# A diagonal LSTM and a quantum convolution on one core: preparation rounds and a part of the first statistics put on ScalarE, aggregation on Pool, and a pause in the circuit's preparation

## The chip, the cores and the metric

The kernel runs on one core of a Trainium2 chip. The metric is the device time of one execution in microseconds (us). Three runs of the kernel before gave 1410.7, 1411.99 and 1412.01 us; their median is 1411.99 us.

## What is computed

The input `x` has 16 images of 128 channels and 64 x 64 pixels, in float32 (33.5 MB). Two layers follow each other, and each adds its result to its input:

```python
x = x + _L0_conv_ref(_gn(x), w_is, b_is, w_ss, b_ss)
x = x + _L1_conv_ref(_gn(x), pre_w, pre_b, q_weights, post_w, post_b)
```

`_gn` is a group norm with 32 groups of 4 channels: mean and variance over 4 channels and all pixels of an image. The first layer is a diagonal LSTM. The rows are skewed (row i shifted right by i), and a scan runs over the 127 diagonals; at each, all rows take one LSTM step in which a row's gates depend on its own state and on that of the row above:

```python
s_s = einsum(w_ss[:, :, 0], h_shift) + einsum(w_ss[:, :, 1], h) + b_ss
o, f, ig = split(sigmoid(gates[:, :3 * C])); g = tanh(gates[:, 3 * C:])
c_new = f * c + ig * g
h_new = o * tanh(c_new)
```

A skewed row is zero where it has no pixel. The second layer projects each pixel's channels to 4 angles, simulates a circuit of 4 qubits with fixed weights, and projects its 4 expectations to 128 channels.

## The kernel before, in words

Channels lie on the partitions. The kernel has three stages, and each engine works through its instructions in the order in which the program issues them, because all three are written under a manual schedule.

**Preparation.** `rows(b)` and `behind(b)` (L247 to L264) issue on SP's queue the loads of image b: 40 rows go into the buffer `ring`, 24 more in three chunks of 512 elements into `rest` or `spare` buffers. `statistics(b, k)` (L285) takes the sums of one chunk of 512 elements on VectorE (`bn_stats`), eight chunks for each image, and `aggregated(b)` (L289) joins the eight into the image's mean and variance per channel (`mv1`, `bn_aggr`). Beside this, 33 rounds of `inv_step` (L190) work out the LSTM states of a row in the steps ahead of its first pixel, where the input is zero and all images and positions have the same state. A round is one chain: 4 matmuls of the state column `hinv[:, j]` with the summed weights `wsT`, 4 gate activations on ScalarE (L202, in the order f, i, g, o), three tiny operations on Pool (L205 `f*c`, L206 `i*g`, L207 their sum, the new cell state in `cinv`), then a tanh (L209) and the product with o (L210) on ScalarE, which gives the next column of `hinv`. After each round two extra matmuls `keep` (L179) run on TensorE with results that nobody reads; the first reads a piece of image b in `ring`. The loop over b (from L375) issues 2 or 3 rounds ahead of the statistics of each image; `between` puts two small weight preparations after the sixth and seventh round.

The end of the preparation, in TensorE's order: Pool copies columns of `hinv` into the first state (L402, L403), 8 matmuls start the gates of step 0 (L408), three `keep` matmuls follow, then the matmul of `group_mean` (L147) with `mv1` of all images, the variance's matmul (L426), and, when VectorE and ScalarE have made `mean1` and `rstd1`, the input matmuls of step 0 (L597).

**The scan.** `step(t)` runs 160 times; rows are handled in two bands of 32, so that a slot that ends a row of the first goes on with a row of the second. A step is three weight products for each of four gates (L783), the sum of two halves (`add`, L798), activations (L802), the cell update (L850 to L861), tanh (L862) and the new state (L868). The input product of a later step (`gate_ps`, L597) stands behind it on TensorE. Pool normalises the input (L576 to L588) and adds the result to `ring` (L641). Beside this VectorE does two side jobs. One is `statistics(us, now)` (L716), which takes from the list `waiting` as many `bn_stats` (L732) of finished rows as fit a budget, for the second norm; `pieces(g)` says at which column a block of four rows comes onto the list: at column 64 for the first eight blocks, in two halves for those of the second band. The other is the circuit's preparation, `steps = circuit(cur)`: 120 small operations (L441, L452, L466, L483) that fill `w_amp`; each step t above 32 draws three of them (`next(steps, None)`, L814 to L816).

**The second layer** runs over the images (L1011 to L1062) and stores the output.

Of the kernel before, what the change touches and what calls it, by code (L numbers as in the profile page):

```python
# [11 lines left out]
F32 = mybir.dt.float32  # L12
AF = mybir.ActivationFunctionType
# [3 lines left out]
P = 128  # L17
NB = 16
NH = 64
NW = 64  # L20
SLOTS = 32
PAIRS = SLOTS // 2
NC = PAIRS * NB
RING = 40
ROWS = 4
BLOCK = ROWS * NW
CHUNK = 2 * BLOCK
EARLY = 33
FIRST = 8
STRIP = 4  # L30
FEW = 96
# [3 lines left out]
BAND = NW + 1  # L35
# [6 lines left out]
GO, GF, GI, GG = 0, 1, 2, 3  # L42
FUNC = {GO: AF.Sigmoid, GF: AF.Sigmoid, GI: AF.Sigmoid, GG: AF.Tanh}
# [38 lines left out]
def kernel(  # L82
# [16 lines left out]
    nc = tc.nc  # L99
# [10 lines left out]
    ring = const.tile([P, NB, RING * NW], F32, name="ring")  # L110
# [21 lines left out]
    w_amp = const.tile([P, 2, 128], F32, name="w_amp")  # L132
# [3 lines left out]
    def place(r):  # L136

        return (r + AHEAD if r < SLOTS else r - SLOTS) * NW
# [21 lines left out]
    small = ctx.enter_context(tc.tile_pool(name="small", bufs=2))  # L160
    with ExitStack() as scan:
# [29 lines left out]
        def inv_step(j, pool):  # L191


            ps = {}
            rhs = hinv[:, j : j + 1].to_broadcast([P, P])
            for g in ORDER:
                ps[g] = pool.tile([P, P], F32, name=f"inv_ps{j}_{g}", tag=f"inv{g}")
                w = wsT[:, g * 128 : (g + 1) * 128]
                nc.tensor.matmul(ps[g], lhsT=w, rhs=rhs, start=True, stop=True)
            ac = small.tile([P, 4], F32, name=f"inv_a{j}", tag="inv_a")  # L200
            for g in ORDER:
                nc.scalar.activation(ac[:, g : g + 1], ps[g][:, 0:1], FUNC[g], bias=bias[:, g : g + 1])  # L202
            ig = small.tile([P, 2], F32, name=f"inv_i{j}", tag="inv_i")
            c = cinv[:, j + 1 : j + 2]
            nc.gpsimd.tensor_mul(ig[:, 0:1], ac[:, GF : GF + 1], cinv[:, j : j + 1])  # L205
            nc.gpsimd.tensor_mul(ig[:, 1:2], ac[:, GI : GI + 1], ac[:, GG : GG + 1])  # L206
            nc.gpsimd.tensor_add(c, ig[:, 0:1], ig[:, 1:2])  # L207
            th = small.tile([P, 1], F32, name=f"inv_t{j}", tag="inv_t")
            nc.scalar.activation(th, c, AF.Tanh)  # L209
            nc.scalar.activation(  # L210
                hinv[:, j + 1 : j + 2], th, AF.Identity, scale=ac[:, GO : GO + 1]
            )

        def above(v, a, b):

# [4 lines left out]
        with ExitStack() as prep:  # L220
# [5 lines left out]
            ps_keep = prep_ps.enter_context(tc.tile_pool(name="ps_keep", bufs=1, space=PSUM))  # L226
# [11 lines left out]
            mv1 = pp.tile([P, NB, 2], F32, name="mv1")  # L238
# [46 lines left out]
            def statistics(b, k):  # L285
                v = ring[:, b, k * CHUNK : (k + 1) * CHUNK] if k < 5 else rests[b][k - 5]
                nc.vector.bn_stats(stats[:, b, k, :], v)

            def aggregated(b):  # L289
                nc.vector.bn_aggr(  # L290
                    mv1[:, b, :], stats[:, b, 0:8].rearrange("p g s -> p (g s)")
                )


            q3 = qw.rearrange("p (n a) -> p a n", a=3)
            ang = pp.tile([P, 2, 3, 8], F32, name="ang")
            rnd = pp.tile([P, 2, 3, 8], F32, name="rnd")
# [73 lines left out]


            between = [angle_weights, output_weights]
            done = 0
            for b in range(NB):  # L375
                while b < NB - 1 and done * (NB - 1) < EARLY * (b + 1):
                    inv_step(done, ps_inv)
                    keep(ps_keep, "keep", ring[:, b, CHUNK : CHUNK + P])
                    keep(ps_keep, "keep", wsT[:, 0:P])
                    if done == 0:  # L380

                        transposed("wxT", wxT, lambda g: wx_n[:, g, :])
                        transposed("w0T", w0T, lambda g: ws_n[g // 2][:, g % 2, 0::2])
                        transposed("w1T", w1T, lambda g: ws_n[g // 2][:, g % 2, 1::2])
                    elif done > 4 and between:
                        between.pop(0)()
                    done += 1
                if b + 2 < NB:
                    rows(b + 2)
                if b + 1 < NB:  # L390
                    behind(b + 1)
                    for k in ORDERED:
                        statistics(b + 1, k)
                for k in (5, 6, 7):
                    statistics(b, k)
                aggregated(b)
            prep_ps.close()


# [20 lines left out]
            var = pp.tile([P, NB], F32, name="var1")  # L420
# [4 lines left out]
            ps = ps_small.tile([P, NB], F32, name="gv1", tag="small")  # L425
# [347 lines left out]
        def step(t, ps):  # L773

            a, b = columns(t)
            few = plain(t)
            a0, b0 = wide(t, LEAST // 2 if few else LEAST)
# [71 lines left out]
            c = cst[:, :, a:w]  # L849
# [21 lines left out]
            s = t + 1  # L871
# [220 lines left out]
    with tc.manual_schedule():  # L1092
# [8 lines left out]
        th = bank(ps_t, "theta1")  # L1101
# [78 lines left out]
```

## Time and profile before

| | us |
|---|---|
| median of three runs | 1411.99 |
| the profiled execution, its own time | 1411.93 |
| its span on the core | 1409.8 |
| preparation, to the first input product of step 0 (L597) | 104.0 |
| start of the first state product (L783) | 106.8 |
| TensorE busy, of the span | 1355.0 (96%) |
| VectorE busy | 975.5 (69%) |
| ScalarE busy | 776.0 (55%) |
| Pool busy | 887.6 (63%) |

The profiled execution's own time is 2.1 us above its span. In what follows a "timeline" is the list of instructions in order of time; its columns are the start in us, the duration in us, the engine, the line, the operation, the tile that is written and those that are read, the shape, the number of merged instructions and, in brackets, the idle time of the engine ahead of it with what ended that. PE is TensorE, DVE VectorE, ACT ScalarE, POOL GpSimd; PEld is TensorE's load of weights. The "chain of waits" goes back from the last instruction, at each step to what released it. A float32 matmul shows as two records.

### The profile page before, as it was taken

What the parts mean: (1) busy time and instruction counts of PE and PEld (TensorE: products, weight loads), DVE (VectorE), ACT (ScalarE), POOL (GpSimd) and SP (SyncE); (2) the same over time, 40 slices, a digit from 0 to 9 for tenths busy, and PEclk for the clock granted to TensorE, in tenths of its full rate; (3) what the DMA queues carried; (4) which work ended last, traced back from release to release, by engine and by line L of the source; (5) the groups of instructions that cost most, each with busy time, mean ns of one, the idle gap of its engine ahead of it and who ended that gap; (6) DMA issues with size and microseconds to landing.
All of it is one profiled execution on the core that took longest, in us unless ns stands there. A gap on an engine that the chain in (4) does not pass through costs nothing.

```text
span 1409.8 us, 20064 instructions
## 1 busy us (share of the span) xinstructions
PE 1355.0 (96%) x6046; PEld 967.6 (69%) x6046; DVE 975.5 (69%) x2541; ACT 776.0 (55%) x1852; POOL 887.6 (63%) x1599
## 2 busy tenths in 40 slices
PE   6778999999999999999999999999999999999995
PEld 5658977777777766666677767777776787886332
DVE  7973565566665666887777776666665567876996
ACT  4655666555555555555555555555555566654331
POOL 4225777777777766777777776777777677763300
PEclk9999999999999999999999999999999999999998
DMA  9960000000000000133333100000000000014999
GB/s 339 407 234 2 1 1 1 1 0 1 0 1 1 1 1 1 60 120 120 120 120 120 60 1 1 1 1 0 1 1 0 1 0 1 1 31 143 383 400 358
DMA packets 64075, 107.04 MB, mean 76 GB/s; under 512 B 5040, under 2 KB 32720, under 8 KB 63968
## 3 DMA queue, kind: packets, MB, share of 16 engines
q1 hardware_dynamic: 59328, 94.39, 18.5%
q0 software_dynamic: 3408, 10.58, 2.0%
q8 instruction: 48, 0.79, 0.2%
q10 hardware_dynamic: 1232, 0.80, 0.2%
q14 instruction: 59, 0.48, 0.1%
HBM read 59.61 MB, written 46.14 MB: 75 GB/s over the span
## 4 chain that ended last, share of the span: by engine, by line
PE 82%; DVE 4%; ACT 1%; issue 1%; POOL 1%; DVEq 0%; ACTq 0%; POOLq 0%
PE ps L783 46%; PE ps L597 28%; PE po_None L1062 3%; PE theta_None L1011 2%; PE am_None L1040 1%; DVE spare L868 1%; DVE ps L858 1%; DVE ps L798 0%; DVE cst L861 0%; DVE stats L732 0%; ACT g L862 0%; ACT g L802 0%; PE po L1062 0%; DVE cst L850 0%; DVE ring L1080 0%
## 5 line engine op out<-in xcount | busy, mean ns | idle before, releaser
L597 PE MATMUL ps<-spare,wxT 128*128 128x512 f32 (+18 forms) x1280 | 479.7, 518 | 0.6 <-POOL spare L588 0.6
L798 DVE TENSOR_TENSOR ps<-ps,both 128x256 f32<-128x256 f32 (+9 forms) x536 | 219.1, 410 | 301.1 <-PE ps L783 299.5
L802 ACT ACTIVATE ps<-ps,bias 128x512 f32<-128x512 f32 (+23 forms) x480 | 279.1, 583 | 221.1 <-DVE ps L798 184.8
L783 PE MATMUL ps<-spare,w1T 128*128 128x256 f32 (+16 forms) x1272 | 346.8, 354 | 9.6 <-DVE spare L759 5.0
L597 PEld LDWEIGHTS ps<-spare,wxT 128*128 128x128 f32 x1280 | 231.1, 190 | 173.0 <-issue 155.4
L783 PE MATMUL ps<-spare,w0T 128*128 128x256 f32 (+16 forms) x1272 | 344.0, 352 | 0.0
L833 ACT COPY both<-ps 128x256 f32<-128x256 f32 (+9 forms) x536 | 189.6, 356 | 181.3 <-PE ps L783 161.7
L783 PEld LDWEIGHTS ps<-spare,w1T 128*128 128x128 f32 x1272 | 230.6, 190 | 36.5 <-DVE spare L868 7.2
L783 PEld LDWEIGHTS ps<-spare,wsT 128*128 128x128 f32 x1088 | 196.1, 190 | 80.4 <-DVE spare L868 30.1
L783 PE MATMUL ps<-spare,wsT 128*128 128x256 f32 (+14 forms) x1088 | 243.9, 366 | 2.6 <-DVE spare L868 1.2
L783 PEld LDWEIGHTS ps<-spare,w0T 128*128 128x128 f32 x1272 | 230.5, 190 | 21.0
L641 POOL TENSOR_TENSOR ring<-ring,spare 128x256 f32<-128x256 f32 (+15 forms) x375 | 231.5, 644 | 17.9 <-DVE spare L868 17.9
L588 POOL TENSOR_TENSOR spare<-spare,rstd 128x512 f32<-128x512 f32 (+10 forms) x160 | 170.9, 1068 | 14.8 <-DVE rstd L158 2.3
L582 POOL TENSOR_TENSOR spare<-ring 128x256 f32<-128x256 f32 (+13 forms) x165 | 139.8, 847 | 0.0
L862 ACT ACTIVATE g<-cst 128x256 f32<-128x256 f32 (+20 forms) x320 | 102.9, 368 | 65.5 <-DVE cst L861 65.1
L868 DVE TENSOR_TENSOR spare<-g,ps 128x256 f32<-128x256 f32 (+17 forms) x319 | 105.3, 368 | 44.8 <-ACT g L862 40.2
L576 POOL TENSOR_TENSOR spare<-ring,mean 128x256 f32<-128x256 f32 (+15 forms) x191 | 122.9, 644 | 5.6 <-DVE mean L148 5.4
L631 POOL TENSOR_TENSOR spare<-spare 128x240 f32<-128x240 f32 (+9 forms) x136 | 102.7, 755 | 36.4 <-DVE spare L868 32.8
L888 POOL COPY spare<-spare 128x16 f32<-128x16 f32 x64 | 21.0, 329 | 150.9 <-DVE spare L868 150.9
L802 ACT ACTIVATE g<-ps,bias 128x512 f32<-128x512 f32 (+20 forms) x160 | 97.3, 608 | 26.6 <-DVE ps L798 20.5
L861 DVE TENSOR_TENSOR cst<-cst,ps 128x256 f32<-128x256 f32 (+20 forms) x320 | 104.6, 368 | 5.5
L858 DVE TENSOR_TENSOR ps<-ps,g 128x512 f32<-128x512 f32 (+20 forms) x160 | 95.0, 594 | 18.8 <-ACT g L802 18.2
(370 smaller groups left out, 1096.4 us busy)
## 6 DMA issues: line engine op xcount, KB each, us to landing
out_dram<-ring SPq DMA_DIRECT2D x93, 256.0 KB, 4.8
ring<-in_x_dram SPq DMA_DIRECT2D x32, 512.0 KB, 7.6
low<-ring SPq DMA_DIRECT2D x6, 2048.0 KB, 7.5
ring<-in_x_dram SPq DMA_DIRECT2D x6, 2048.0 KB, 8.1
spare<-in_x_dram SPq DMA_DIRECT2D x27, 256.0 KB, 6.3
rest<-in_x_dram SPq DMA_DIRECT2D x21, 256.0 KB, 6.4
ring<-low POOLq DMA_DIRECT2D x18, 256.0 KB, 6.7
ring<-in_x_dram SPq DMA_DIRECT2D x16, 256.0 KB, 7.1
```

What stands on the lines that cost most here:

```text
L576: op = nc.gpsimd.tensor_sub(by_pairs(xn, 0, j0, j1), x0, over(mean1, j1 - j0))
L582: op = nc.gpsimd.tensor_sub(by_pairs(xn, 1, j0, j1), lower, of)
L588: nc.gpsimd.tensor_mul(v, v, r)
L597: nc.tensor.matmul(ps[g][:, :, a:b], lhsT=wxT[:, g * 128 : (g + 1) * 128], rhs=xns[t % 2][:, :, a:b], start=t > 0, stop=True, skip_group_c ...
L641: op = engine.tensor_add(x1, x1, by_pairs(new, q, j0, j1))
L783: nc.tensor.matmul(out, lhsT=w[:, g * 128 : (g + 1) * 128], rhs=rhs, start=False, stop=True, skip_group_check=True,)
L798: nc.vector.tensor_add(v, v, both[g][:, a:b])
L802: nc.scalar.activation(to[:, :, a:w], ps[g][:, :, a:w], FUNC[g], bias=bias[:, g : g + 1])
L833: nc.scalar.copy(both[g][:, a:b], ps[g][:, 0, a:b])
L858: nc.vector.tensor_mul(ig, ig, act[GG][:, :, a:w])
L861: nc.vector.tensor_add(c[:, q], c[:, q], ig[:, q])
L868: nc.vector.tensor_mul(new[:, q, a:v], th[:, q, a:v], act[GO][:, q, a:v])
```

## The change

Four things are changed. In `inv_step` the products `i*g` and the sum move from Pool to one ScalarE activation (scale i, bias `f*c`); Pool keeps `f*c`, now issued right after the gate f. For images 1 to 4 (`aside`) the chunk k = 0 is no longer taken by `bn_stats` but by two ScalarE activations with accumulated sums (`moments_of`), issued after the rounds of that image, and a third that writes the mean. For images 1 to 12 `bn_aggr` is left out, and Pool joins the eight entries of four images at a time (`gathering`), in pieces of which one is issued after each round (`some`); what is left when the rounds are over is issued after the loop over the images. And the circuit draws its three operations at the steps 33 to 62 and from 106 on, instead of from 33 on without a pause. Two smaller edits go with it: `coefficients()` is issued later on Pool, and the first `keep` after a round reads `wsT` instead of `ring`.

```diff
+GATHER = 4
@@ inv_step
+            kept = small.tile([P, 1], F32, name=f"inv_k{j}", tag="inv_k")
+            c = cinv[:, j + 1 : j + 2]
...
             for g in ORDER:
-                nc.scalar.activation(ac[:, g : g + 1], ps[g][:, 0:1], FUNC[g], bias=bias[:, g : g + 1])
-            ig = small.tile([P, 2], F32, name=f"inv_i{j}", tag="inv_i")
-            c = cinv[:, j + 1 : j + 2]
-            nc.gpsimd.tensor_mul(ig[:, 0:1], ac[:, GF : GF + 1], cinv[:, j : j + 1])
-            nc.gpsimd.tensor_mul(ig[:, 1:2], ac[:, GI : GI + 1], ac[:, GG : GG + 1])
-            nc.gpsimd.tensor_add(c, ig[:, 0:1], ig[:, 1:2])
...
+                activate(ac[:, g : g + 1], ps[g][:, 0:1], FUNC[g], bias=bias[:, g : g + 1])
+                if g == GF:
+                    nc.gpsimd.tensor_mul(kept, ac[:, GF : GF + 1], cinv[:, j : j + 1])
+            activate(c, ac[:, GG : GG + 1], AF.Identity, scale=ac[:, GI : GI + 1], bias=kept)
+            activate(th, c, AF.Tanh)
+            activate(hinv[:, j + 1 : j + 2], th, AF.Identity, scale=ac[:, GO : GO + 1])
@@ preparation
+            aside = range(1, 1 + GATHER)
...
+            def moments_of(b):
+                at = place(SLOTS)
+                v, x0 = ring[:, b, at : at + CHUNK], ring[:, b, at : at + 1]
+                junk = ps_small.tile([P, CHUNK], F32, name=f"junk{b}", tag="small")
+                for k, func in enumerate((AF.Identity, AF.Square)):
+                    nc.scalar.activation(
+                        junk, v, func, bias=x0, scale=-1.0, accum_out=sums1[:, k, b : b + 1]
+                    )
+                nc.scalar.activation(
+                    entries[:, b, 0:2, 1],
+                    sums1[:, 0, b : b + 1].to_broadcast([P, 2]),
+                    AF.Identity,
+                    bias=x0,
+                    scale=-1.0 / CHUNK,
+                )
+
+            def gathering(b0):
...
+                if b0 in aside:
+                    nc.gpsimd.tensor_mul(s1, s1, s1)
+                    nc.gpsimd.tensor_scalar_mul(s1, s1, -0.5 / CHUNK)
+                    yield
+                    nc.gpsimd.tensor_scalar_mul(s2, s2, 0.5)
+                    nc.gpsimd.tensor_add(
+                        inners[:, :, 0:2], *(v.unsqueeze(2).to_broadcast(pair) for v in (s1, s2))
+                    )
+                    yield
...
+                def total(to, v):
+                    n = 8
+                    while n > 1:
+                        nc.gpsimd.tensor_add(gathered[:, :, 0:n], v[:, :, 0:n], v[:, :, n : 2 * n])
+                        v, n = gathered, n // 2
+                        yield
+                    nc.gpsimd.tensor_add(to.unsqueeze(2), v[:, :, 0:1], v[:, :, 1:2])
+                    nc.gpsimd.tensor_scalar_mul(to, to, 1.0 / 16)
+                    yield
+
+                yield from total(m, means)
+                nc.gpsimd.tensor_sub(gathered, means, m.unsqueeze(2).to_broadcast([P, GATHER, 16]))
+                nc.gpsimd.tensor_mul(gathered, gathered, gathered)
+                yield
+                nc.gpsimd.tensor_scalar_mul(within, inners, 1.0 / BLOCK)
+                nc.gpsimd.tensor_add(gathered, gathered, within)
+                yield
+                yield from total(var, gathered)
...
-            coefficients()
             for v in (*hst, *xns, none):
                 nc.gpsimd.memset(v, 0.0)
             nc.gpsimd.memset(w_image, 0.0)
 
             for k in (3, 4, 0):
                 statistics(0, k)
+            coefficients()
...
+            behind_pool = []
+
+            def some():
+                for later in behind_pool[:1]:
+                    if next(later, True) is not None:
+                        behind_pool.pop(0)
+
             for b in range(NB):
                 while b < NB - 1 and done * (NB - 1) < EARLY * (b + 1):
                     inv_step(done, ps_inv)
-                    keep(ps_keep, "keep", ring[:, b, CHUNK : CHUNK + P])
+                    some()
+                    keep(ps_keep, "keep", wsT[:, 0:P])
                     keep(ps_keep, "keep", wsT[:, 0:P])
...
+                if b in aside:
+                    moments_of(b)
...
                     for k in ORDERED:
-                        statistics(b + 1, k)
+                        if k or b + 1 not in aside:
+                            statistics(b + 1, k)
                 for k in (5, 6, 7):
                     statistics(b, k)
-                aggregated(b)
+                if b in (0, *range(13, NB)):
+                    aggregated(b)
+                if b in (5, 9, 13):
+                    behind_pool.append(gathering(b - GATHER))
+            for later in behind_pool:
+                for _ in later:
+                    pass
             prep_ps.close()
@@ step
-            if t > SLOTS:
+            if SLOTS < t < BAND - 2 or t > BAND + RING:
                 for _ in range(3):
                     next(steps, None)
```

More of the change, by code (lines that the diff above doesn't have):

```diff
@@ L200, in inv_step, with activate @@
             ac = small.tile([P, 4], F32, name=f"inv_a{j}", tag="inv_a")
-            for g in ORDER:
-                nc.scalar.activation(ac[:, g : g + 1], ps[g][:, 0:1], FUNC[g], bias=bias[:, g : g + 1])
-            ig = small.tile([P, 2], F32, name=f"inv_i{j}", tag="inv_i")
-            c = cinv[:, j + 1 : j + 2]
-            nc.gpsimd.tensor_mul(ig[:, 0:1], ac[:, GF : GF + 1], cinv[:, j : j + 1])
-            nc.gpsimd.tensor_mul(ig[:, 1:2], ac[:, GI : GI + 1], ac[:, GG : GG + 1])
[L207 to L212, printed above, removed]
+            kept = small.tile([P, 1], F32, name=f"inv_k{j}", tag="inv_k")
+            c = cinv[:, j + 1 : j + 2]
+            th = small.tile([P, 1], F32, name=f"inv_t{j}", tag="inv_t")
+            def activate(to, v, func, **of):
+                nc.scalar.activation(to, v, func, **of)
+            for g in ORDER:
+                activate(ac[:, g : g + 1], ps[g][:, 0:1], FUNC[g], bias=bias[:, g : g + 1])
[4 more added lines that the diff above has]
+            activate(hinv[:, j + 1 : j + 2], th, AF.Identity, scale=ac[:, GO : GO + 1])
         def above(v, a, b):
@@ L292, in aggregated @@
                 )
+            entries = stats[:, :, 0:8].rearrange("p b g (h s) -> p b (g h) s", s=3)
+            aside = range(1, 1 + GATHER)
+            sums1 = w_amp[:, 1, 0 : 2 * NB].rearrange("p (k i) -> p k i", i=NB)
+            gathered, within = (
+                w_amp[:, 0, k * P // 2 : (k + 1) * P // 2].rearrange("p (i e) -> p i e", i=GATHER)
+                for k in range(2)
+            )
[14 more added lines that the diff above has]
+                )
@@ new lines, in gathering @@
+            def gathering(b0):
+                b1 = b0 + GATHER
+                pair = [P, GATHER, 2]
+                means, inners = entries[:, b0:b1, :, 1], entries[:, b0:b1, :, 2]
+                s1, s2 = (sums1[:, k, b0:b1] for k in range(2))
+                if b0 in aside:
[5 more added lines that the diff above has]
+                        inners[:, :, 0:2], *(v.unsqueeze(2).to_broadcast(pair) for v in (s1, s2))
+                    )
+                    yield
+                m, var = (mv1[:, b0:b1, k] for k in range(2))
+                def total(to, v):
[15 more added lines that the diff above has]
+                yield from total(var, gathered)
```

## The prediction

> **What bounds the kernel now.** I read the page's busy lines first, then the slices, then the timeline of the preparation, then the chain of waits of the scan. TensorE is busy for 96% of the span, so little but the ends can be won; the change works at one end, the first 104 us. There three things run beside each other: loads, statistics, rounds. The question is which is last at the group mean's matmul. One round, from the timeline of 88 to 125 us:
>
> ```profile
> 88.24 1.16 PE L199 MATMUL inv_ps<-hinv,wsT 128*128 128x128 f32 x8 [0.46 <-ACT hinv L210]
> 88.77 0.93 ACT L202 ACTIVATE inv_a<-inv_ps,bias 128x1 f32<-128x1 f32 x4 [0.58 <-PE inv_ps L199]
> 89.17 0.19 POOL L205 TENSOR_TENSOR inv_i<-inv_a,cinv 128x1 f32<-128x1 f32 x1 [1.54 <-ACT inv_a L202]
> ...
> 89.83 0.19 POOL L207 TENSOR_TENSOR cinv<-inv_i 128x1 f32<-128x1 f32 x1
> 90.05 0.20 ACT L209 ACTIVATE inv_t<-cinv 128x1 f32<-128x1 f32 x1 [0.35 <-POOL cinv L207]
> ...
> 90.29 0.29 ACT L210 ACTIVATE hinv<-inv_t,inv_a 128x1 f32<-128x1 f32 x1
> 90.63 1.16 PE L199 MATMUL inv_ps<-hinv,wsT 128*128 128x128 f32 x8 [0.46 <-ACT hinv L210]
> ```
>
> The period is 90.63 - 88.24 = 2.39 us; nearly all 33 rounds have it, and only ScalarE, Pool and TensorE are in it. The end of the preparation:
>
> ```profile
> 94.17 0.37 DVE L290 BATCH_NORM_AGGREGATE mv<-stats 128x2 f32<-128x48 f32 x1
> ...
> 95.07 0.29 ACT L210 ACTIVATE hinv<-inv_t,inv_a 128x1 f32<-128x1 f32 x1
> ...
> 95.42 0.19 POOL L402 COPY spare<-hinv 128x1 f32<-128x1 f32 x1 [0.49 <-ACT hinv L210]
> 95.54 0.18 POOL L403 COPY spare<-hinv 128x1 f32<-128x1 f32 x1
> ...
> 100.48 0.40 PE L147 MATMUL gm<-mv,wide_sb 128*128 128x16 f32 x2
> ```
>
> The reader is to see that the last aggregation ends at 94.54, and that the group mean's matmul comes 5.9 us later. What holds it is TensorE's own queue: the rounds end at 95.36, Pool copies the state, 8 matmuls (L408) run from 95.78, the three `keep` from 97.67. VectorE has 5.9 us to spare here, although it is full before. The path is rounds, Pool's copies, TensorE.
>
> In the scan a step takes 8.61 us and TensorE sets it. The chain of waits leaves it for VectorE in one place:
>
> ```profile
> 583.09 4.33 PE ps L783 x20
> ...
> 592.00 2.03 DVE amp L452 x3
> 594.03 0.32 DVE stats L732
> ...
> 600.89 5.45 PE ps L783 x24
> ...
> 645.10 5.18 PE ps L783 x24
> ```
>
> Seven steps take 62.01 us instead of 60.27: 1.7 us are lost where the circuit (L452) and the statistics of the first rows (L732) meet.
>
> [...] the tanh without a pointer 203 ns, the product with one 294 ns. [...] the eight records of a round took 2.05 us at 11.21, after little work, and 1.16 us later. [...] a Pool instruction that needs the one before starts 0.08 us after its end (L206 to L207, 89.74 to 89.83), one that doesn't starts 0.05 ahead of it.
>
> **The change part by part.**
>
> *The round on ScalarE.* Removed from the path: L206, L207 and their hops. From the gate g's end (89.48, the third of four activations spaced by 0.22) to the tanh's start it is 0.57 us now. Added: one activation with two pointers, queued behind the gate o, which starts at 89.44. By the overlap it starts at 89.61, [...] and the tanh follows by the 0.03 that L210 keeps behind L209: 90.03 instead of 90.05. Gain 0.02 us for each round, 33 rounds: -0.7. Bounds: if it takes no more than the 0.294 of L210, the gain is 0.12, in all -3.9; if it starts only at o's end (89.70), it loses 0.07: +2.4. `f*c` on Pool ends at 89.36 and isn't late.
>
> *The sums on ScalarE.* Four times three activations stand in the same queue, between a round's L210 and the next round's gates. The nearest rows of 128 x 512 are 0.66 (L802, with a pointer) and 0.63 (L1031, from the same memory, without): I take 0.70 each. [...] The third takes 0.29. With overlaps the next gate may start -0.09 + 0.75 + 0.03 + 0.75 - 0.09 + 0.29 - 0.09 = 1.55 us after L210's end; now it starts after 0.58, the wait for TensorE, which hides that much. So each delays the chain by 0.97; the second stands behind a copy of weights (33.35 to 33.62, the gate at 33.77) that has used up 0.4 of the cover. Together +4.3 (3.5 to 5.5). Their chunks have landed: images 1 to 4 by about 15, 20, 27 and 32 us, the sums come after 25, 32, 38 and 43.
>
> *VectorE.* It loses 4 chunks of 0.67 and 12 aggregations of 0.37 us, 7.1 us in all, off the path: nothing. The loads also limit it: the last of them is issued at 87.07, those before it took 6.4 us to land, so the last chunk comes at about 93.5 and statistics can't end before that. They free buffers a little earlier, but the DMA engines are full from 20 to 90 us (mean share 1.03).
>
> *Pool's aggregation.* In the order of the built program each piece stands behind a round's `f*c`, beside the round's ScalarE time: at most 1 us of a period of 2.39, nothing. But of 32 pieces 19 are issued with rounds (the first four images join the queue after round 14). 21 Pool instructions stand behind the last round's `f*c`, and **behind them the three copies of the state, for which TensorE waits**. Prices from Pool's rows: 128 x 64 product by a number 0.37 (L713), two operands 0.32 (L714), 128 x 32 0.25 (L588, L711), 128 x 16 0.22 (L576), 8 and 4 wide 0.20 (L313, L332), scaling of 4 at most 0.20 (L304). A `total` is 0.25 + 0.22 + 3 x 0.20 + 5 x 0.08 = 1.47; three are left, 4.4. The difference and squares of four images are 0.32 + 0.32 + 0.37 + 0.32 + 0.2 for waits = 1.5; the rest of the group before is 0.72. Sum 6.6 us. The last `f*c` ends 1.1 us after its round's start (93.95 + 0.19 against 93.02), so Pool is free at 7.7, the copies end at 8.2, and L408 starts at 8.2 after the round's start, now at 2.76: +5.5 us (4.3 without part of the waits, 6.2 if stepped patterns are slower). It is met again nowhere: group mean, `rstd1` and step 0 follow TensorE's queue.
>
> *TensorE in that hole.* It is idle from the last `keep` (1.9 after the round's start) to 8.2, over 6 us, [...] Bounds 0, and +3.5 with the three `keep` slow too.
>
> *The pause.* The circuit's 120 draws, 3 for a step, now end at step 115. The 1.7 us above go, but 30 draws meet the half rows of the second band at steps 106 to 115, with the same budget (nine `bn_stats` of 0.28 us) in about four of them. I take 1.4 of 1.7 as coming back: -0.3 (-1.8 to +0.7).
>
> *`coefficients` later, `keep` on `wsT`*: nothing. Pool does the same work before the first round's product (15.17) in both orders, and no wait of TensorE for a load shows in the waits from 15 to 96.
>
> Sum: -0.7 + 4.3 + 5.5 + 1.8 - 0.3 = +10.6 us on the profiled execution's own 1411.93 (span 1409.8 and 2.1 around it; 0.06 below the median, which doesn't matter): 1422.5, say 1422.
>
> **The rivals.** (a) *Faster, since the statistics set the end.* VectorE is over 99% busy from 40 to 80 us; if the group mean waited for it, its 7.1 us would come off: 1405. It decides if the loads of L408 could be issued ahead of 94.5. Against: the 5.9 us after the last aggregation, and the loads' landing. 7%. (b) *No change*: the activation with two pointers costs 0.29 us and ScalarE's rounds give 3.9 back, which pays for the sums, and Pool's tail is mostly hidden: 1411.93 - 3.9 + 4.3 = 1412. Against: every dependent pair of Pool rows shows its 0.08. 7%. (c) *The tail is cheap, the sums are not*: slower by the sums and rounds alone, -0.7 + 4.3 - 0.3: 1415. 12%. (d) *TensorE stays slow through the `keep`s and Pool's stepped patterns cost more*: 1428. 6%. My forecast: 68%.
>
> **How the numbers follow.** Its own terms: low ends together +1.5 or so, high ends +18; independent, they give about 3 us on either side, 1418 to 1426. The range goes down to (c) and up to (d), leaving out (a) and (b): 1415 to 1428. A measurement of this kernel tells about 0.2%, 2.8 us, from no change. Faster: (a), and a part of (b): 0.08. Within 0.2%: the rest of (b), a part of (c): 0.09. Slower: 0.83.
>
> **What would show it.** Right: rounds of about 2.37 us; four gaps ahead of the gates that are longer by 1 us; Pool busy without a break for 6 to 7 us after the last `f*c`, and the copies of `hinv` behind it; the first L408 of its kind at 104 to 106 us with records twice as far apart; the first input product of step 0 at about 115; steps of 8.61 us from 63 to 105. Wrong: the copies within 1 us of the rounds' end, rounds below 2.3 us, or a group mean whose last wait is for VectorE.

## The result, and the profile after

| | before | after |
|---|---|---|
| median of six runs, us | 1411.38 | 1421.49 |
| lowest and highest, us | 1410.7 to 1412.01 | 1419.73 to 1422.55 |
| the profiled execution's own time, us | 1411.93 | 1421.89 |
| its span, us | 1409.8 | 1420.1 |

The changed kernel is slower: the ratio of the times is 1.007, with an interval of 1.0057 to 1.0083. A later repetition of it had one execution of 1466.49 us at a lower granted clock (0.942 against 0.991 to 0.993), which is left out of the times below. In what follows lines of the changed kernel stand under their new numbers: the rounds' matmul is L200 (was L199), all ScalarE work of a round L207, `f*c` L212, Pool's aggregation L328 to L353, the copies of the state L482 and L483 (L402, L403), the gate matmuls of step 0 L488 (L408), `keep` L183 (L182), the group mean's matmul L148 (L147), the first input product L677 (L597), the state products L863 (L783).

First two lines of the kernel before that the prediction describes without showing them, the first of the eight gate matmuls of step 0:

```profile
95.78 0.49 PE L408 MATMUL ps<-spare,w1T 128*128 128x128 f32 x2 [0.83 <-POOL spare L403]
...
96.10 0.39 PE L408 MATMUL ps<-spare,w0T 128*128 128x128 f32 x2
```

The timeline of the changed kernel's last rounds and of the end of its preparation, to be laid beside these and beside the two timelines that the prediction shows:

```profile
94.80 1.16 PE L200 MATMUL inv_ps<-hinv,wsT 128*128 128x128 f32 x8 [0.42 <-ACT hinv L207]
95.32 0.93 ACT L207 ACTIVATE inv_a<-inv_ps,bias 128x1 f32<-128x1 f32 x4 [0.58 <-PE inv_ps L200]
95.66 0.19 POOL L212 TENSOR_TENSOR inv_k<-inv_a,cinv 128x1 f32<-128x1 f32 x1 [1.70 <-ACT inv_a L207]
...
96.15 0.38 ACT L207 ACTIVATE cinv<-inv_a,inv_k 128x1 f32<-128x1 f32 x1
96.56 0.20 ACT L207 ACTIVATE inv_t<-cinv 128x1 f32<-128x1 f32 x1
96.79 0.29 ACT L207 ACTIVATE hinv<-inv_t,inv_a 128x1 f32<-128x1 f32 x1
97.05 0.37 DVE L293 BATCH_NORM_AGGREGATE mv<-stats 128x2 f32<-128x48 f32 x1
97.14 1.16 PE L200 MATMUL inv_ps<-hinv,wsT 128*128 128x128 f32 x8 [0.42 <-ACT hinv L207]
...
98.15 0.41 POOL L352 TENSOR_SCALAR w_amp<-stats 128x64 f32<-128x64 f32 x1
...
99.14 0.29 ACT L207 ACTIVATE hinv<-inv_t,inv_a 128x1 f32<-128x1 f32 x1
...
104.80 0.22 POOL L345 TENSOR_SCALAR mv<-mv 128x4 f32<-128x4 f32 x1
105.08 0.32 POOL L482 COPY spare<-hinv 128x16 f32<-128x16 f32 x2
105.34 0.18 POOL L483 COPY spare<-hinv 128x1 f32<-128x1 f32 x1
105.57 0.79 PE L488 MATMUL ps<-spare,w1T 128*128 128x128 f32 x2 [6.50 <-POOL spare L483]
106.16 0.64 PE L488 MATMUL ps<-spare,w0T 128*128 128x128 f32 x2
...
109.14 1.36 PE L183 MATMUL I-1382_1383<-rest,wsT 128*128 128x384 f32 x2
...
112.50 0.39 PE L148 MATMUL gm<-mv,wide_sb 128*128 128x16 f32 x2
...
116.20 2.05 PE L677 MATMUL ps<-spare,wxT 128*128 128x128 f32 x16 [0.64 <-POOL spare L668]
```

A round now takes 97.14 - 94.80 = 2.34 us. The last state column is there at 99.43, and nothing on TensorE or ScalarE keeps it from being used; but Pool works from 98.15 to 105.02, 6.87 us, on its own queue alone (no wait there names another engine), and copies the column only then. This stretch of aggregation behind the last round is called the tail below, and the idle time that it leaves on TensorE the hole. TensorE waits 6.50 us for that copy (the bracket of the first L488), and comes back slow: two matmuls of L488 stand 106.58 - 106.16 = 0.42 us apart, where before two stood 96.33 - 96.10 = 0.23 apart. The windows of the changed kernel show the same (columns: window, length, busy us and count of PE, PEld, DVE, ACT, POOL, then the granted clock, the DMA share and GB/s):

```profile
98.00:105.00 7.00, 1.01 (x7) 0.63 (x5) 0.00 (x0) 2.65 (x7) 5.47 (x22) 0.89 0.00 1
100.00:110.00 10.00, 4.43 (x18) 3.91 (x18) 0.00 (x0) 0.73 (x1) 4.32 (x19) 0.67 0.00 0
```

VectorE has nothing to do in either window, and the clock is 0.67 over the second window. By stage, from the two timelines, each difference being after less before:

| stage | before | after | difference |
|---|---|---|---|
| last round starts | 93.02 | 97.14 | +4.12 |
| from there to the first gate matmul of step 0 | 2.76 | 8.43 | +5.67 |
| from there to the group mean's matmul | 4.70 | 6.93 | +2.23 |
| from there to the first input product | 3.50 | 3.70 | +0.20 |
| from there to the first state product | 2.82 | 2.88 | +0.06 |
| scan, from there to the first state product of the last step | 1172.97 | 1171.17 | -1.80 |
| rest of the span | 130.08 | 129.83 | -0.25 |

The sum is +10.2 of the 10.3 us by which the spans differ. The chain of waits over the steps where the circuit met the first statistics now has TensorE alone:

```profile
594.98 5.18 PE ps L863 x24
600.16 3.43 PE ps L677 x8
603.60 5.18 PE ps L863 x24
...
655.28 5.18 PE ps L863 x24
```

Seven steps take 655.28 - 594.98 = 60.30 us, where seven took 62.01.

### The profile page after: what moved, and what is told of

Its sections match the earlier page's. It is cut to its first block, busy times and chain, and to the rows that moved or that the text cites. A ratio compares the mean times of both kernels' runs of the same rounds, so it can differ in the third digit from the quotient of the medians.

```text
span 1420.1 us, 20084 instructions
## 1 busy us (share of the span) xinstructions
PE 1358.7 (96%) x6046; PEld 969.9 (68%) x6046; DVE 976.4 (69%) x2525; ACT 790.7 (56%) x1905; POOL 885.0 (62%) x1579
## 4 chain that ended last, share of the span: by engine, by line
PE 83%; DVE 3%; ACT 1%; issue 1%; POOL 1%; DVEq 0%; ACTq 0%; POOLq 0%
PE ps L863 47%; PE ps L677 29%; PE po_None L1141 3%; PE theta_None L1090 2%; PE am_None L1119 1%; DVE spare L948 1%; DVE ps L938 0%; DVE stats L812 0%; PE po L1141 0%; DVE cst L941 0%; ACT g L882 0%; DVE ps L878 0%; DVE ring L1159 0%; ACT g L942 0%; ACT ps L882 0%
## 5 line engine op out<-in xcount | busy, mean ns | idle before, releaser
L677 PE MATMUL ps<-spare,wxT 128*128 128x512 f32 (+18 forms) x1280 | 479.7, 518 | 0.6 <-POOL spare L668 0.6
L863 PE MATMUL ps<-spare,w1T 128*128 128x256 f32 (+16 forms) x1272 | 346.6, 354 | 9.1 <-DVE spare L839 4.8
L677 PEld LDWEIGHTS ps<-spare,wxT 128*128 128x128 f32 x1280 | 230.9, 190 | 173.2 <-issue 155.5
L863 PE MATMUL ps<-spare,w0T 128*128 128x256 f32 (+16 forms) x1272 | 343.8, 352 | 0.0
L863 PEld LDWEIGHTS ps<-spare,w1T 128*128 128x128 f32 x1272 | 230.4, 190 | 36.1 <-DVE spare L948 6.9
L863 PEld LDWEIGHTS ps<-spare,wsT 128*128 128x128 f32 x1088 | 195.6, 190 | 79.7 <-DVE spare L948 32.7
L863 PE MATMUL ps<-spare,wsT 128*128 128x256 f32 (+14 forms) x1088 | 244.0, 366 | 1.6 <-DVE spare L948 1.4
L863 PEld LDWEIGHTS ps<-spare,w0T 128*128 128x128 f32 x1272 | 230.3, 190 | 21.2
```

The costliest lines, as they stand in the source:

```text
L677: nc.tensor.matmul(ps[g][:, :, a:b], lhsT=wxT[:, g * 128 : (g + 1) * 128], rhs=xns[t % 2][:, :, a:b], start=t > 0, stop=True, skip_group_c ...
L863: nc.tensor.matmul(out, lhsT=w[:, g * 128 : (g + 1) * 128], rhs=rhs, start=False, stop=True, skip_group_check=True,)
```

## The experiments

My theory was that of the prediction: Pool's leftover pieces in front of the copies, the clock that falls in the hole, and the sums in ScalarE's queue. The rivals were that the statistics set the end, and that the tail is only a face of something else (a late load, a slow copy). "Before" is the time of the kernel before on the same chip; each ratio is to that.

**The copies ahead of the leftover.** The loop that issues what is left of the aggregation goes behind the three copies; nothing else moves.

```diff
-            for later in behind_pool:
-                for _ in later:
-                    pass
             prep_ps.close()
...
             nc.gpsimd.tensor_copy(hst[0][:, 1, NB : NB + 1], hinv[:, EARLY : EARLY + 1])
+            for later in behind_pool:
+                for _ in later:
+                    pass
             first = {}
```

> The changed kernel, with Pool's three copies of the state issued ahead of the aggregation that is left over after the rounds. Theory (the leftover stands ahead of the copies, and TensorE's queue waits for them): the first gate matmuls start 2.8 us after the last round's start instead of 8.4, TensorE doesn't cool down, and the group mean's matmul is then held by Pool's aggregation at about 8.7 us after the last round's start instead of 15.4: 1421.5 - 6.7 = 1414.8 us. Rival (the statistics or the landing of the loads set the end of the preparation): the order on Pool is of no account, 1421.5.

Measured: 1412.84 us, ratio 1.0009 (1.0002 to 1.0016), against 1.007 for the changed kernel: some 8.6 us come back by a change of order alone. Its timeline:

```profile
98.59 0.19 POOL L479 COPY spare<-hinv 128x1 f32<-128x1 f32 x1 [0.39 <-ACT hinv L207]
...
98.94 0.49 PE L488 MATMUL ps<-spare,w1T 128*128 128x128 f32 x2 [0.78 <-POOL spare L480]
...
103.69 0.37 PE L148 MATMUL gm<-mv,wide_sb 128*128 128x16 f32 x2
...
104.60 0.25 POOL L345 TENSOR_SCALAR mv<-mv 128x4 f32<-128x4 f32 x1
```

The first L488 comes 98.94 - 96.23 = 2.71 us after the last round's start (2.76 before the change), and the group mean's matmul 4.75 after that (4.70 before), with the gate matmuls 0.22 us apart (99.27 and 99.49) where the changed kernel has 0.42: the tail is off the path and the slow pace is gone. Pool does the same 21 instructions, 19 of them now behind the copies, to 104.85, while TensorE works. I had expected 1414.8, since the group mean would wait for Pool's last number. It doesn't: that matmul reads the means alone, and the variances, which come last, are first read at 104.88 on VectorE, just after they are ready. This shows the tail's cause, and that it is the place in the queue, not Pool's work, which costs.

**The hole filled.** Five more `keep` matmuls stand in TensorE's hole; they need nothing from Pool.

```diff
             ps_gate = scan.enter_context(tc.tile_pool(name="ps_gate", bufs=7, space=PSUM))
...
+            for _ in range(5):
+                keep(ps_gate, "gate", wxT[:, 0 : 4 * P])
```

> The changed kernel, with five matmuls of 512 columns that nobody reads put on TensorE behind the last round, 5.5 us of work in the 6.5 us in which it is idle. Theory (TensorE's clock falls in the hole): the eight gate matmuls and the first of the three that follow run at full pace again, 1.7 + 0.5 us less, 1419.3 us. Rival (their slow pace is of another cause, or the hole alone costs): 1421.5.

Measured: 1419.01 us, ratio 1.0053 (1.0038 to 1.0068).

```profile
103.79 0.49 PE L490 MATMUL ps<-spare,w1T 128*128 128x128 f32 x2 [1.83 <-POOL spare L485]
104.11 0.39 PE L490 MATMUL ps<-spare,w0T 128*128 128x128 f32 x2
...
108.48 0.40 PE L148 MATMUL gm<-mv,wide_sb 128*128 128x16 f32 x2
```

The way from the first gate matmul to the group mean is 4.69 us, as before the change (4.70), instead of 6.93, with Pool's tail as it was (8.44 us from the last round to the first gate matmul). The matmuls stand 104.33 - 104.11 = 0.22 us apart. So the slow clock is a term of its own, 2.2 us, and it is gone when TensorE's idle time there is filled down to 1.83 us. The profile shows this; the ratios alone, 1.0053 here and 1.007 with the hole, have intervals that overlap.

**No sums on ScalarE.** VectorE takes all chunks again; Pool still aggregates, with two pieces fewer.

```diff
-            aside = range(1, 1 + GATHER)
+            aside = ()
```

> The changed kernel, with the chunk k = 0 of images 1 to 4 taken by VectorE's statistics again, so that no sums stand in ScalarE's queue; Pool's aggregation stays for images 1 to 12, three pieces shorter, of which the tail after the rounds loses some four instructions. Theory (each sum delays the next round's gates by 0.9 to 1.3 us, and one round runs with a slow TensorE for the same reason): 3.9 + 0.6 us less on the rounds and 0.9 us less tail, 1416.1 us. Rival (the sums hide in ScalarE's idle time): only the shorter tail, 1420.6.

Measured: 1414.56 us, ratio 1.0018 (1.0011 to 1.0025). The intervals between rounds, here and below from one new state column to the next, are 2.34 or 2.35 us but for three (3.40, 2.39 and 2.90), and the last round starts at 91.17. The tail is still there, 7.21 us from the last round's start to the first L488, and so is the slow pace, 99.39 - 98.97 = 0.42 us from one gate matmul to the next:

```profile
98.38 0.80 PE L488 MATMUL ps<-spare,w1T 128*128 128x128 f32 x2 [5.28 <-POOL spare L483]
98.97 0.63 PE L488 MATMUL ps<-spare,w0T 128*128 128x128 f32 x2
```

The medians are 6.9 us apart, more than the 5.4 that I had expected. The profiles show about 4 of it as the sums' delays (below), 0.3 as a later gap and 1.2 as the two pieces that they add to Pool's tail (8.43 against 7.21 us). The last 1.4 this run doesn't settle: the slow stretch behind the hole is 0.8 shorter (6.10 us from the first gate matmul to the group mean, against 6.93), but the changed kernel without its pause, in which nothing else of the preparation differs, has 6.59 in one profile and 6.99 in another. VectorE has its four chunks back, and nothing is seen to be lost by that.

**One group on Pool instead of three.** The images 5 to 12 are aggregated by VectorE again, so that the queue of pieces is empty before the rounds end.

```diff
-                if b in (0, *range(13, NB)):
+                if b not in aside:
                     aggregated(b)
-                if b in (5, 9, 13):
+                if b == 5:
                     behind_pool.append(gathering(b - GATHER))
```

> The changed kernel, with Pool's aggregation for images 1 to 4 only, which ends with the rounds, and images 5 to 12 aggregated on VectorE as before. Theory (Pool's tail is the largest term, VectorE has time to spare): 5.7 us of tail and 2.2 us of slow TensorE go, VectorE's 8 x 0.37 us more don't matter: 1413.6 us. Rival (VectorE's relief is worth something, the tail is not what costs): 1421 or more.

Measured: 1412.16 us, ratio 1.0006 (0.9998 to 1.0014).

```profile
95.31 1.16 PE L200 MATMUL inv_ps<-hinv,wsT 128*128 128x128 f32 x8 [0.41 <-ACT hinv L207]
...
98.02 0.49 PE L488 MATMUL ps<-spare,w1T 128*128 128x128 f32 x2 [0.78 <-POOL spare L483]
```

The first L488 comes 98.02 - 95.31 = 2.71 us after the last round's start. With a second way to remove it the tail costs the same: it is the leftover, nothing that the first edit may have moved beside it.

**The new round alone**, put into the kernel before:

```diff
-            nc.gpsimd.tensor_mul(ig[:, 0:1], ac[:, GF : GF + 1], cinv[:, j : j + 1])
-            nc.gpsimd.tensor_mul(ig[:, 1:2], ac[:, GI : GI + 1], ac[:, GG : GG + 1])
-            nc.gpsimd.tensor_add(c, ig[:, 0:1], ig[:, 1:2])
...
+                if g == GF:
+                    nc.gpsimd.tensor_mul(kept, ac[:, GF : GF + 1], cinv[:, j : j + 1])
+            activate(c, ac[:, GG : GG + 1], AF.Identity, scale=ac[:, GI : GI + 1], bias=kept)
```

> The kernel before, with one part of the change alone: the cell state of a preparation round comes from one ScalarE activation instead of two Pool operations. Theory (the profile of the changed kernel shows 2.35 us for an undisturbed round, against 2.39): 33 x 0.045 = 1.5 us less, 1409.9 us. Rival (the prediction's own estimate, 0.02 us a round): 1410.7.

Measured: 1409.19 us, before 1411.86, ratio 0.9981 (0.9973 to 0.999). Rounds take 2.34 or 2.35 us instead of 2.39: 1.4 us over the rounds. The scan is 0.5 us shorter as well (1172.46 against 1172.97), of which I had expected nothing: steps 8, 19 and 156 take 0.28 us less each. They do so in every profile with the new round and in none without it; what links them with the round is open. Another 0.9 us of the difference of the two profiles is in the first interval between rounds alone (3.40 against 4.33), which also differs between executions of one and the same order of instructions (3.47 in the profile of the pause alone, below, whose preparation is that of the kernel before). So the new round is worth 1.4 us by its own rows and 0.5 in the scan; the median's 2.7 may hold a share of that chance, and how much is open.

**The pause alone**, put into the kernel before:

```diff
-            if t > SLOTS:
+            if SLOTS < t < BAND - 2 or t > BAND + RING:
```

> The kernel before, with the pause of the circuit's preparation alone. By the steps of the changed kernel 1.3 to 1.8 us less: 1409.9 us. By the prediction's term, 0.3 less: 1411.1.

Measured: 1410.15 us, ratio 0.9989 (0.9983 to 0.9996), 1.7 us faster. Against steps of 8.61 us the scan loses 0.4 us over steps 61 to 73 (1.8 before), and 0.5 over 105 to 116 (nothing before). The 0.4 are two steps, 64 and 65, of 8.86 and 8.72; such a pair stands at steps 94 and 95 in the profile before and at 90 and 91 in the changed kernel's, so I count it as no part of what the pause does. By the steps, then, the pause gains 1.8 and loses 0.5: 1.3 us.

**The change without its pause**, the opposite edit, twice: once with the first runs, once beside a repetition of the changed kernel on the same chip.

```diff
-            if SLOTS < t < BAND - 2 or t > BAND + RING:
+            if t > SLOTS:
```

> The changed kernel, with the circuit's preparation drawn from step 33 on without a pause. The prediction's term for the pause was -0.3 us, so 1421.8; the profile of the changed kernel shows steps of 8.61 us from 61 to 89 and only 0.5 us lost at 110 to 115, against 1.8 us lost at 65 to 73 before, so by the steps 1422.8.

> The changed kernel itself, to stand on the same chip beside the next one, since the run without the pause lay within the spread of the changed kernel: 1421.5 us.

> The changed kernel without the pause again, beside it. By the steps (1.1 to 1.3 us lost at 65 to 73 more than at 110 to 115) and by the pause alone in the kernel before (1.7 us less): 1.2 to 1.7 us more than the changed kernel, 1422.9. By the prediction's term: 0.3 more.

Measured: 1421.28 us (ratio 1.0068, 1.0053 to 1.0083) the first time, which tells nothing beside a changed kernel timed elsewhere. On one chip: with the pause 1420.93 (1.0061, 1.0047 to 1.0074), without it 1422.11 (1.0071, 1.0059 to 1.0083). The intervals overlap, so the medians' 1.2 us alone settle nothing; the profiles do: the scan takes 1171.31 with the pause and 1172.33 without (1172.26 the first time), and the chain of waits of the run without it leaves TensorE where the kernel before did:

```profile
601.88 2.03 DVE amp L532 x3
...
604.49 0.60 DVE stats L812 x2
...
637.55 1.87 DVE w_amp L563 x3
...
640.00 0.76 DVE stats L812 x3
```

**The mean ahead of the gates.** In the kernel before, the two matmuls of the group norm go ahead of the copies' consumers in TensorE's queue, and the `keep` around them are dropped. This asks where the rival of the statistics would begin to be true.

```diff
+            group_mean(ps_small, mv1[:, :, 0], mean1, 1, 1.0)
...
+            nc.tensor.matmul(ps, lhsT=group, rhs=var, start=True, stop=True)
...
             first = {}
...
-            for v in (rests[NB - 2][0], rests[NB - 2][2], rests[NB - 1][0]):
-                keep(ps_small, "small", v[:, 0 : 3 * P])
-
-            group_mean(ps_small, mv1[:, :, 0], mean1, 1, 1.0)
```

> The kernel before, with the group mean's and the variance's matmuls issued on TensorE ahead of the eight gate matmuls of step 0, and without the matmuls that only keep TensorE busy after the rounds. Theory (TensorE's queue holds the group mean for 5.9 us after the last aggregation): the mean's matmul starts at about 95 us instead of 100.5, and the first input product of step 0 at about 98.5 instead of 104.0: 1411.4 - 5.5 = 1405.9 us. Rival (the statistics or the loads are what is late): 1411 or more.

Measured: 1406.28 us, ratio 0.9963 (0.995 to 0.9975).

```profile
95.87 0.37 DVE L290 BATCH_NORM_AGGREGATE mv<-stats 128x2 f32<-128x48 f32 x1
...
96.30 0.40 PE L147 MATMUL gm<-mv,wide_sb 128*128 128x16 f32 x2 [1.84 <-DVE mv L290]
...
98.20 0.64 PE L416 MATMUL ps<-spare,w0T 128*128 128x128 f32 x2
...
101.19 2.08 PE L591 MATMUL ps<-spare,wxT 128*128 128x128 f32 x16
```

Here, and in no run with the old order, the bracket at the group mean names VectorE's last aggregation: with the gate matmuls out of the way the statistics are last. The median gains 5.6 us. The profiled execution is the slowest of the five, 1408.84 us: its last aggregation ended at 96.24 (94.54 in the kernel before), and the mean came only just behind it, 4.2 us earlier than before; the input product kept 2.8 of that (101.19 against 103.98), since the gate matmuls now stand between, and ran slow (98.63 - 98.20 = 0.43 us apart) after idle times of 1.84 and 0.89 us.

**The good parts without the three `keep`.** The kernel before with the new round and the pause, and without the three `keep` between the gate matmuls and the group mean. Only the last part of the edit is shown; the two others stand above.

```diff
-            for v in (rests[NB - 2][0], rests[NB - 2][2], rests[NB - 1][0]):
-                keep(ps_small, "small", v[:, 0 : 3 * P])
```

> The kernel before with the round on ScalarE, the pause, and without the three matmuls between the gate matmuls of step 0 and the group mean's, which only keep TensorE busy. Theory (each term stands for itself; TensorE's queue holds the mean until the rounds end no longer than the statistics do): rounds -2.0, pause -1.6, and the mean's matmul at the later of 95.7 (gate matmuls) and the last aggregation (94.5 to 96.2), some 2.5 us sooner: 1411.6 - 6.1 = 1405.5 us. Rival (the clock falls without the three, or the terms hide each other): 1408 or more.

Measured: 1404.53 us against 1411.57, ratio 0.995 (0.9938 to 0.9962): faster than both kernels.

```profile
93.88 0.37 DVE L292 BATCH_NORM_AGGREGATE mv<-stats 128x2 f32<-128x48 f32 x1
93.90 0.49 PE L410 MATMUL ps<-spare,w1T 128*128 128x128 f32 x2 [0.79 <-POOL spare L405]
...
95.79 0.29 PE L147 MATMUL gm<-mv,wide_sb 128*128 128x16 f32 x2
...
99.19 2.05 PE L596 MATMUL ps<-spare,wxT 128*128 128x128 f32 x16 [0.65 <-POOL spare L587]
```

TensorE waits 0.79 us for the copies and not again until the mean; the gate matmuls keep their distance (0.22 us, 94.22 and 94.45), and the 2.8 us of the three `keep` (97.67 to 100.48 before) are gone. With 1.9 to 2.7 from the new round and 1.3 to 1.7 from the pause the parts make 6.0 to 7.2; measured are 7.0. The three `keep` were not taken out alone, so their 2.8 is read from the timeline.

**The same, with VectorE relieved.** Pool aggregates images 1 to 4 during the rounds and leaves nothing over; `aside` is empty. The edit is to the changed kernel.

```diff
-            aside = range(1, 1 + GATHER)
+            aside = ()
...
-                if b in (0, *range(13, NB)):
+                if b not in range(1, 1 + GATHER):
                     aggregated(b)
-                if b in (5, 9, 13):
+                if b == 5:
                     behind_pool.append(gathering(b - GATHER))
...
-            for v in (rests[NB - 2][0], rests[NB - 2][2], rests[NB - 1][0]):
-                keep(ps_small, "small", v[:, 0 : 3 * P])
```

> The one before, with Pool's aggregation for images 1 to 4 (without ScalarE's sums), which ends with the rounds. VectorE then has 4 x 0.37 = 1.5 us less work, and now its end is near the path: if the statistics set the group mean here, up to 0.5 us less than the one before, as long as the loads have landed; if the gate matmuls do, the same.

Measured: 1405.08 us, ratio 0.9951 (0.9938 to 0.9964), no different from the run ahead of it. The group mean follows the gate matmuls directly at 95.96 in this one too, so an earlier end of the statistics has nothing to give; nor did they end earlier (95.52, against 94.25 in the run ahead of it).

## Why the prediction was right

The forecast was 1422, the median is 1421.49, and its path (rounds, Pool's copies, TensorE) is the one that the timeline shows. Step by step, measured sizes from the profiles:

- *The round on ScalarE*: -0.7 was predicted, 0.02 for each round. The new activation takes 0.38 us (mean 0.378); the estimate was 0.39. Two rows of the profile before give nearly the same, the tanh without a pointer (L209, 0.203) and the product with one (L210, 0.294): 0.203 + 2 x (0.294 - 0.203) = 0.385, within 0.01 of the 0.378. But it begins 1.35 after the round's start, when the estimate had 1.37 (89.61 - 88.24): it starts 0.10 ahead of the last gate's end (95.32 + 0.93 against 96.15), where the estimate had 0.09. And the tanh begins at 1.76 instead of 1.79. A round gains 0.045 us, 1.4 in all; the sign and the cause were right, the size was half. The further 0.5 us in the scan, which comes with the new round, wasn't foreseen.
- *The sums on ScalarE*: +4.3 was predicted. Three of the four delay a round by 0.88 us (3.23 instead of 2.35) and one, behind a copy of weights, by 1.31: together 3.95. The price of the accumulation stood in the sum as 0.05 (0.75 where the activation alone was put at 0.70), a guess of mine that no row of the profile before shows; it is a row of its own, which hides partly:

```profile
28.26 0.67 ACT L311 ACTIVATE junk<-ring 128x512 f32<-128x512 f32 x1
28.87 0.18 ACT L311 ACTIVATION_READ_ACCUMULATOR junk<-ring 128x1 f32 x1
29.09 0.69 ACT L311 ACTIVATE junk<-ring 128x512 f32<-128x512 f32 x1
29.72 0.19 ACT L311 ACTIVATION_READ_ACCUMULATOR junk<-ring 128x1 f32 x1
29.81 0.28 ACT L314 ACTIVATE stats<-w_amp,ring 128x2 f32<-128x2 f32 x1
30.00 0.69 ACT L207 ACTIVATE inv_a<-inv_ps,bias 128x1 f32<-128x1 f32 x4
```

  From the end of a round's last product (28.35) to the next gate it is 1.65 us, where the sum had 1.55. Its overlap of 0.09 is there: the first activation starts at 28.26, as in the profile before a copy started at 16.25 while L210 ended at 16.05 + 0.29 = 16.34. The delay is nevertheless 0.88 and not 1.07, as the four gates then find their matmuls done and take 0.69 us instead of 0.93: the prediction had left that out, and the two misses nearly cancel. A later interval of 2.61 (+0.26, in every profile with the sums) wasn't foreseen, and its cause is open; nor was one of 2.96 (+0.61) in the profiled execution. In that one TensorE ran slow behind the longest wait for the sums (1.77 us for the eight records, the granted clock 0.60 from 38.20 to 40.00 us), which the repetition of the same kernel passed in 1.16:

```profile
38.20 1.77 PE L200 MATMUL inv_ps<-hinv,wsT 128*128 128x128 f32 x8 [1.73 <-ACT hinv L207]
```

```profile
38.21 1.16 PE L200 MATMUL inv_ps<-hinv,wsT 128*128 128x128 f32 x8 [1.73 <-ACT hinv L207]
```

- *Pool's tail*: +5.5 was predicted, +5.67 measured. Twenty-one instructions took 6.87 us, predicted 6.6: the small prices held, the 64 wide product by a number takes 0.41 instead of 0.37. Both runs that empty Pool's queue ahead of the copies come back to 2.71 us, from 8.43.
- *The clock in the hole*: +1.8 was predicted, an estimate of mine that no row of the profile before shows; +2.2 was measured. The gate matmuls take 3.57 instead of 1.89 us (the granted clock was 0.50 from 105.50 to 109.10, and 1.00 before from 95.70 to 97.60), and the first `keep` behind them is slow for a part (1.36 us against 0.81), which had been kept for the upper bound. The run with the hole filled shows this term by itself.
- *The pause*: the step that failed in size. -0.3 was predicted, since 1.4 of 1.7 us would come back at steps 106 to 115; 0.5 came back, and by the steps the pause is worth -1.3. The half rows of the second band put a smaller load on VectorE than full ones (1.82 us of `bn_stats` in the fullest step there against 2.04), and the overrun that remains, four steps of 8.72 to 8.75 against 8.61, is about a quarter of what steps 65 to 73 lost (8.67 to 9.36). By the medians the pause alone gives -1.7 and the pair on one chip -1.2, both within the prediction's -1.8 to +0.7. The scan of the changed kernel is 1.8 us shorter, but the 0.5 of the new round is in that.
- *VectorE's relief*: nothing, as predicted. It didn't even bring VectorE's own end forward (97.42, against 94.54 before): from 20 to 98 us VectorE's `bn_stats` wait 7.8 us for loads, against 1.3 before. Rival (a), the statistics at the end, is refuted for the changed kernel's order by the timeline (VectorE's last aggregation ends at 97.42, the mean's matmul comes at 112.50), and it comes true only in the order of the run with the mean ahead of the gates: its turning point is the queue of TensorE. Rival (b) needed the rounds to give 3.9 and the tail to be hidden, (c) a cheap tail; neither was so. Of (d), the slow first `keep` was true, 0.56 us of it, and is in the clock's 2.2.
- Not foreseen: 0.2 us between the group mean and the input product (3.70 against 3.50). Its cause is open; every profile with Pool's aggregation has 0.1 to 0.2 of it, that with one group too.

Rounds and sums make 4.1 where the prediction had 3.6; in that are 0.4 by which the first round began late (11.59 against 11.21; with the old preparation it began at 11.54 and 11.84 in two other profiles, so that is chance) and 0.6 of the slow TensorE. The tail made 5.7 for 5.5, the clock in the hole 2.2 for 1.8, the pause -1.3 for -0.3; the rest of the scan (-0.5) and of the span (-0.25) and the 0.26 behind the group mean stood for nothing. That these misses cancel is why the total is within 0.5 us, and that is luck: single terms were off by up to 1.0. The mechanism, Pool's tail ahead of the copies and the clock behind it, was right, and its two terms are 7.9 of the 10.2 us.

## What to carry to other kernels

Before work is moved to an idle engine, look at what that engine still has to do at the end of the stage, and for whom: 6.9 us of small Pool operations cost 7.9 us ahead of three copies, and nothing that the timeline shows behind them. An engine that is full may still be off the path, and relief is worth something only once nothing else is queued ahead of the consumer; ask first which queue the consumer stands in. Work that exists to keep a clock up has a price as well, 2.8 us for three matmuls here: when it stands ahead of the consumer and the hole is short (0.79 us in the run without the three), try without it.

## What the hardware showed that I had not expected

In the changed kernel each of the eight activations with an accumulated sum is followed by a row of its own, ACTIVATION_READ_ACCUMULATOR, of 0.18 to 0.19 us, which in the first overlaps the end of the activation by 0.06 us (28.26 + 0.67 against 28.87).

The first interval between rounds is 3.4 to 3.5 us in some executions and 4.3 to 4.5 in others, with the old round and with the new one: the eight records of the second round are slow in the longer one. The repetition of the changed kernel and the one without its pause, whose preparations are the same, on the same chip:

```profile
18.29 1.91 PE L200 MATMUL inv_ps<-hinv,wsT 128*128 128x128 f32 x8
```

```profile
17.93 1.06 PE L200 MATMUL inv_ps<-hinv,wsT 128*128 128x128 f32 x8
```

So about 1 us of any difference between two single profiles can be chance. What makes the records slow in one execution and not in another, here and in the two rounds at 38.2 us shown above, no run shows. The granted clock was 0.60 over the changed kernel's slow records (38.20 to 40.00 us), but the profile before has 1.00 from 17.80 to 19.70, where the eight records of the second round took 1.91 us, so it names no cause there.

TensorE also ran slow without a pause as long as the hole: in the run with the mean ahead of the gates, after 1.84 us of idle time and another of 0.89, the matmuls stood 0.43 us apart, while after 0.79 us in the run without the three `keep` they stood 0.22 apart. The length of one pause doesn't settle it: after 1.83 us, in the run with the hole filled, they stood 0.22 apart as well, and after 1.73 us the eight records of a round took 1.77 us in one execution of the changed kernel and 1.16 in another. What does settle it is open.
